# A graph kernel's first SAGE pass: two of eight blocks of adjacency rows multiplied by their mask on VectorE, and layer norm's scaling moved to ScalarE

## The chip, the cores and the metric

The kernel runs on 1 core of a Trainium2 chip. The time is that of one execution on the device, in microseconds (us). The engines are called as in the profile: PE is TensorE (matmuls; PEld its weight loads), DVE is VectorE, ACT is ScalarE, POOL is GpSimd, SP is SyncE, which here only issues transfers. Each engine works through its own instructions strictly in the order in which they are written; engines wait for each other through semaphores.

## The reference

Two graph layers are run on 16 graphs of 1024 nodes with 128 features. The first is a gated graph network of four steps. The second, cut to what matters:

```python
x = _layernorm(x + gated(x, adj, mask))       # end of the first layer
adj_d = adj * keep                            # keep: row by row, some neighbours are struck out, and their mirror images too
deg = clip(sum(adj_d, -1), 1)
out = (adj_d @ x / deg) @ Wr1 + x @ Wx1 + b1  # the first of three SAGE passes
h1  = batch_norm(relu(out / norm(out)))
# the sum adj_d @ h1 for the second pass is taken in the same sweep; two more passes and a head follow
```

adj holds zeros and ones. keep is stored as a matrix nr ("not removed") of zeros and ones, one for each graph, in which row i says what row i has struck out. Entry (i, j) of adj_d is 1 when adj, nr at (i, j) and nr at (j, i) are all 1.

## The kernel before

The program has four stages: the gated layer woven together with the search for removed neighbours (to about 1323 us), the first SAGE pass (Sage.first, about 1323 to 1893 us), the second pass, and the third pass with the head. The change is in the first pass alone.

The first pass walks over the graphs b in 16 slots each (method slot, t = 0 to 15), whose order is written out by hand; nothing is rescheduled. In one turn of 16 slots, graph n = b + 1 is prepared while graph b is multiplied. A batch here means one such turn. What a slot holds of the work that the prediction names:

- **unit(n, t)**, L1469, every slot. It makes a piece of 128 rows by 512 columns of the transposed adj_d. With f = t // 8 and j = t % 8, PE adds up in PSUM (p_u, two buffers) one 512-wide matmul of nr (L1477) and, for each of four row blocks k = 4f + i, a turned block of adj (L1483) and a turned block of nr (L1484), each a 128x128 bf16 matmul with the identity. ACT then writes relu(sum - 2) as p_at (L1485): 1 only where all three are 1. "Unit 8" is unit(n, 8), and "Relu 8" its L1485.
- **pack**, L1492: POOL casts each p_at to bytes (p_b).
- **agg**, L1556: eight 512-wide matmuls over p_at; for x in slots 0, 1, 3, 4, for the new features r in slots 9, 10, 12, 14.
- **evict**, L1562, ACT: in slots 2 and 5 the two sums over x leave PSUM (s_ag). "Evict 2" and "evict 5" below.
- **degrees**, slots 2 and 5: L1541 on DVE and L1542 on ACT read the degree row out of s_ag. **degree_columns**, slots 3 and 6: four tiny matmuls (L1549) turn it into PSUM tile s_tr, and DVE reads it there (L1551, L1552). s_tr has one buffer, so the next to write it waits for L1551.
- **out_first**, slots 5 and 7, PE; **scale_rows**, slots 6 and 8, DVE (L1376, L1377); **squares**, ACT (L1384, L1385); **rows**, slots 7 and 9, DVE (L1390 to L1395); **split**, ACT L1400 and POOL L1401; **turn_r**, slots 11 and 13, PE L1406, ACT L1592, DVE L1593.
- **norm_stats**, slots 0 and 1: DVE statistics of x of graph n (L1510, L1512), the root on ACT (L1515), the reciprocal on DVE (L1516). **norm**, slots 2 and 3: four DVE instructions each (L1522), x - mean times 1/deviation, in place. **turn_x**, slots 6 and 8: PE turns four blocks of x each into s_tr (L1406).
- **check(n, k)**, L1501: DVE tests that a block of adj holds only 0 and 1; each block is f32, 128x1024, and all of it is read. Blocks 4 to 7 in slots 4, 5, 10, 11, and blocks 0 to 3 of the graph after in slots 12 to 15.

Within a slot, what belongs to graph b is written ahead of what belongs to graph n, except unit. On DVE, slots 5 and 6 stand thus: L1541, the check of block 5, L1376, L1377, L1551, L1552. On PE, slot 6 is unit 6, L1549, turn_x, and the last waits for L1551.

Of the kernel before, what the change touches and what calls it, by code (L numbers as in the profile page):

```python
# [8 lines left out]
F32 = mybir.dt.float32  # L9
BF = mybir.dt.bfloat16  # L10
# [4 lines left out]
AF = mybir.ActivationFunctionType  # L15
ALU = mybir.AluOpType
# [5 lines left out]
P = 128  # L22
# [3 lines left out]
NB = N // P  # L26
# [357 lines left out]
def sage_layers(ctx, tc, cst, adj, mask, not_r, summed, x1, W, vec, Wl, bl, out):  # L384
# [106 lines left out]
    with ExitStack() as c1:  # L491
# [7 lines left out]
        for b in range(B):  # L499
# [3 lines left out]
            for f in range(2):  # L503
                t = nrp.tile([P, 4, N], BF, name="a_nr")
                nc.sync.dma_start(t, rows_of(not_r[b][f * HF:(f + 1) * HF, :]))
                nr.append(t)
            norm(s, s)
            nc.sync.dma_start(rows_of(x1[b]), s)
            ht = [transposed(lambda i: s[:, 4 * f + i, :], "s_t4",
# [70 lines left out]
    with ExitStack() as c3:  # L580
        ld = pool("c_ld", c3, bufs=2)
        psp = pool("c_psp", c3, bufs=2, space=PSUM)
        for b in range(B):
            s = ld.tile([P, NB, C], F32, name="c_x")
            nc.sync.dma_start(s, rows_of(x1[b]))
            ht = normed(b)
            project(2, b, ht, psp)
            for f in range(2):
                pt = ps2.tile([P, 4, P], F32, name="s_tr")
                for i in range(4):  # L590
                    nc.tensor.transpose(pt[:, i, :], acc[b][f][:, i * P:(i + 1) * P], ident)
                for i in range(4):
                    k = 4 * f + i
                    m = cst["mask"][:, k, b:b + 1]
                    y = wk.tile([P, C], F32, name="c_y")
                    nc.vector.scalar_tensor_tensor(y, pt[:, i, :], m, blb, op0=ALU.mult, op1=ALU.add)
                    nc.vector.scalar_tensor_tensor(s[:, k, :], y, m, s[:, k, :],
                                                   op0=ALU.mult, op1=ALU.add)
            norm(s, s)
            nc.sync.dma_start(rows_of(out[b]), s)  # L600
# [596 lines left out]
class Sage:  # L1197
# [14 lines left out]
    def __init__(self, ctx, tc, cst, adj, not_r, summed, nodemask, W, vec, Wl, bl, out, bad):  # L1212
# [27 lines left out]
        self.wxp = one.tile([C, 2, C], F32, name="s_wxp")  # L1240
        self.r6 = one.tile([6, 2 * C], BF, name="s_r6")

    def load_given(self):

        nc = self.nc
        nodemask, W, vec, Wl, bl = self.given
        for i in range(3):
            nc.sync.dma_start(self.wr[:, i, :], W[2 * i])
            nc.sync.dma_start(self.wx[:, i, :], W[2 * i + 1])
        nc.sync.dma_start(self.wl, Wl.rearrange("(k c) e -> c k e", c=C))  # L1250
        row = lambda v: v.rearrange("(o c) -> o c", o=1)
        for i, v in enumerate(vec):
            nc.sync.dma_start(self.vr[i:i + 1, :], row(v))
        nc.sync.dma_start(self.vr[9:, :], row(bl))
        self.m48 = self.wk.tile([P, NB, C], F32, name="p_rh", bufs=1).rearrange("p a b -> p (a b)")[:3 * B, :]
        for i in range(3):
            nc.sync.dma_start(self.m48[i * B:(i + 1) * B, :], nodemask)

    def constants(self):

        nc, ident, K = self.nc, self.cst["ident"], 3 * B
        const = self.const
        self.one16 = const([1, 1], 1.0, "s_one16", F16)

        self.sel01 = const([10, 3, 6], 0.0, "s_sel01")
        for i in range(3):
            nc.vector.tensor_copy(self.sel01[:, i, 3:], ident[:10, 3 * i:3 * i + 1].to_broadcast([10, 3]))
        self.ones = const([6, P], 1.0, "s_ones", BF)
        nc.vector.tensor_add(self.part6, ident[:6, 0:3], ident[:6, 3:6])
        self.part48 = const([K, 3], 1.0, "s_part48")  # L1270
        for base, m in ((0, 1), (B - 1, -1)):
            nc.gpsimd.affine_select(self.part48, self.part48, pattern=[[-m * B, 3]], compare_op=ALU.is_ge,
                                    fill=0.0, base=base, channel_multiplier=m)
        nc.vector.tensor_add(self.graph, ident[:K, :B], ident[:K, B:2 * B])
        nc.vector.tensor_add(self.graph, self.graph, ident[:K, 2 * B:K])
        nc.vector.memset(self.r6[:, C:], 0.0)

        mask, junk = self.cst["mask"], self.wxp[:, 0, :].rearrange("p (a b) -> p a b", a=NB)
        nc.vector.scalar_tensor_tensor(junk, mask, 0.0, mask, op0=ALU.is_gt, op1=ALU.not_equal,
                                       accum_out=self.bad[:, BAD - 1:BAD])  # L1280

        drop = self.wr2
        nc.vector.tensor_copy(drop, ident)
        nc.vector.memset(drop[:1, :], -1.0)
        nc.vector.memset(drop[:1, :1], 0.0)
        nc.vector.memset(self.mask48[:B, :], 1.0)
# [13 lines left out]
    def const(self, shape, v, name, dt=F32):  # L1300
        t = self.one.tile(shape, dt, name=name)
        self.nc.vector.memset(t.bitcast(F32) if dt is FR else t, v)
        return t
# [165 lines left out]
    def unit(self, b, t):  # L1469

        nc, g, f, j = self.nc, self.g[b], t // 8, t % 8
        if t == 0:
            g["at"] = self.atp[b % 2].tile([P, NB, N], FR, name="p_at")
        cols = slice(f * HF, (f + 1) * HF)
        ib, nr = self.cst["ident_b"], g["nr"]
        pu = self.ps2.tile([P, HF], F32, name="p_u")
        nc.tensor.matmul(pu, ib, nr[:, j, cols], start=True, stop=False)  # L1477
        for i in range(4):
            k = 4 * f + i

            a = g["a", k].bitcast(BF).rearrange("p (n h) -> p n h", h=2)
            blk = slice(j * P, (j + 1) * P)
            nc.tensor.matmul(pu[:, i * P:(i + 1) * P], a[:, blk, 1], ib, start=False, stop=False)  # L1483
            nc.tensor.matmul(pu[:, i * P:(i + 1) * P], nr[:, k, blk], ib, start=False, stop=(i == 3))  # L1484
        nc.scalar.activation(g["at"][:, j, cols], pu, AF.Relu, bias=self.less2)  # L1485
# [8 lines left out]
    def check(self, b, k):  # L1494

        if b >= B:
# [4 lines left out]
        self.nc.vector.scalar_tensor_tensor(low, a, 0.0, a, op0=ALU.is_gt, op1=ALU.not_equal,  # L1501
                                            accum_out=self.bad[:, c:c + 1])

    def norm_stats(self, b, f):
        nc, g = self.nc, self.g[b]
        if f == 0:
            g["mv"] = self.small.tile([P, NB, 2], F32, name="p_mv")
        st = self.small.tile([P, 4, 6], F32, name="p_st")
        for i in range(4):
            nc.vector.bn_stats(st[:, i, :], g["s"][:, 4 * f + i, :])  # L1510
        for i in range(4):
            nc.vector.bn_aggr(g["mv"][:, 4 * f + i, :], st[:, i, :])  # L1512
        if f == 1:
            g["rs"] = self.small.tile([P, NB], F32, name="p_rs")
            nc.scalar.activation(g["rs"], g["mv"][:, :, 1], AF.Sqrt, bias=self.eps)  # L1515
            nc.vector.reciprocal(g["rs"], g["rs"])  # L1516

    def norm(self, b, f):
        nc, g = self.nc, self.g[b]
        for i in range(4):  # L1520
            k = 4 * f + i
            nc.vector.tensor_scalar(g["s"][:, k, :], g["s"][:, k, :], g["mv"][:, k, 0:1], g["rs"][:, k:k + 1],  # L1522
                                    op0=ALU.subtract, op1=ALU.mult)

    def split_x(self, b, f):
        self.split(f, self.g[b]["s"][:, 4 * f:4 * f + 4, :], self.xh, self.xl, 1)
# [68 lines left out]
    def slot(self, b, t):  # L1595

        nc, g, n = self.nc, self.g.get(b), b + 1
# [23 lines left out]
        if now:  # L1621
# [3 lines left out]
            if t in (0, 1, 3, 4):  # L1625
                f, lo = t // 3, t in (1, 4)
# [5 lines left out]
            if t in (6, 8):  # L1632
                f = t // 8
# [3 lines left out]
            if t in (7, 9):  # L1637
                f = t // 9
# [15 lines left out]
        if nxt:  # L1654
            if t < 2:
                self.norm_stats(n, t)
            if t in (2, 3):
                self.norm(n, t - 2)
            if t in (6, 8):
                self.turn_x(n, t // 8)  # L1660
            if t in (7, 12):
                self.split_x(n, t // 12)
            if t < 4 and not now:
                self.check(n, t)
            if t in (4, 5, 10, 11):
                self.check(n, (4, 5, 10, 11).index(t) + 4)
            if t >= 12:
                self.check(n + 1, t - 12)

# [202 lines left out]
    def last(self, r48):  # L1872
        nc, tc, cst = self.nc, self.tc, self.cst
        with ExitStack() as c:
# [64 lines left out]
            for b in range(B + 1):  # L1939
                if b < B:  # L1940
                    head(b)
                if b:
                    norm(b - 1)
# [102 lines left out]
```

## Time and profile before

| | |
|---|---|
| median of 9 runs | 2365.28 us (2358.18 to 2365.91) |
| the profiled execution | 2363.19 us, of it the span from first to last instruction 2361.0 us |
| PE busy over the span | 96% |
| DVE, ACT, POOL busy over the span | 81%, 58%, 44% |
| the first SAGE pass | about 1323 to 1893 us |
| one steady batch of it (L1551 of slot 6 to the next) | 33.72 us |

All instruction times below are those of the one profiled execution; a line of the timeline gives start, duration, engine, source line, operation and tiles, and in brackets how long the engine had been idle and who released it. Durations on one engine overlap a little, so distances are taken from start to start.

### The profile page before, as it was taken

What the parts mean: (1) busy time and instruction counts of PE and PEld (TensorE: products, weight loads), DVE (VectorE), ACT (ScalarE), POOL (GpSimd) and SP (SyncE); (2) the same over time, 40 slices, a digit from 0 to 9 for tenths busy, and PEclk for the clock granted to TensorE, in tenths of its full rate; (3) what the DMA queues carried; (4) which work ended last, traced back from release to release, by engine and by line L of the source; (5) the groups of instructions that cost most, each with busy time, mean ns of one, the idle gap of its engine ahead of it and who ended that gap; (6) DMA issues with size and microseconds to landing.
All of it is one profiled execution on the core that took longest, in us unless ns stands there. A gap on an engine that the chain in (4) does not pass through costs nothing. (4 is left out here: it accounts for less than half of the span.)

```text
span 2361.0 us, 35730 instructions
## 1 busy us (share of the span) xinstructions
PE 2267.9 (96%) x11945; PEld 1563.4 (66%) x11945; DVE 1905.8 (81%) x4132; ACT 1371.7 (58%) x3206; POOL 1028.7 (44%) x964
## 2 busy tenths in 40 slices
PE   6999999999999999999999799999999999998987
PEld 4665655666656666656565577777777778886865
DVE  4998998998989989989899878777777566665777
ACT  3556565656465655555664565665666545555756
POOL 3235254263262452543532556666666435551002
PEclk9999999999999999999999899999999999998989
DMA  7327244363362362633640777778777277764414
GB/s 264 113 97 264 73 171 170 115 233 126 105 209 102 127 239 69 207 133 117 233 134 25 267 292 292 273 264 296 282 273 268 107 266 248 245 217 163 127 37 145
DMA packets 214406, 436.18 MB, mean 185 GB/s; under 512 B 59586, under 2 KB 80740, under 8 KB 214212
## 3 DMA queue, kind: packets, MB, share of 16 engines
q1 hardware_dynamic: 186244, 345.70, 42.0%
q0 software_dynamic: 23040, 83.90, 10.1%
q10 hardware_dynamic: 4928, 4.21, 0.6%
q8 instruction: 96, 1.57, 0.3%
q14 instruction: 98, 0.80, 0.1%
HBM read 324.49 MB, written 109.25 MB: 184 GB/s over the span
## 5 line engine op out<-in xcount | busy, mean ns | idle before, releaser
L1092 PE MATMUL h_g<-h_h,h_wh 128*128 128x512 f32 x768 | 397.8, 600 | 3.1 <-DVE h_r L1105 3.0
L1092 PE MATMUL h_g<-h_ms,h_wi 128*128 128x512 f32 x768 | 392.2, 592 | 0.0
L1492 POOL CAST p_b<-p_at 128x512 uint8<-128x512 f32 x256 | 258.0, 1028 | 121.8 <-ACT p_at L1485 121.8
L735 DVE TENSOR_TENSOR_SCAN f_rank<-f_a,f_first,f_pd 128x1024 f16<-128x1024 f32 x128 | 299.3, 2344 | 3.3
L1080 PE MATMUL h_g<-h_a,h_hi 128*128 128x512 f32 x1024 | 284.3, 418 | 5.9 <-DMA h_a<-in_adj_dram 5.7
L1092 PEld LDWEIGHTS h_g<-h_ms,h_wi 128*128 128x128 f32 x768 | 145.7, 190 | 183.8 <-issue 161.3
L1121 POOL TENSOR_TENSOR h_h<-h_zh,h_r 128x512 f32<-128x512 f32 x126 | 181.8, 1443 | 195.0 <-DVE h_r L1120 172.9
L1080 PE MATMUL h_g<-h_a,h_lo 128*128 128x512 f32 x1024 | 264.3, 395 | 0.0
L1485 ACT ACTIVATE p_at<-p_u,s_less 128x512 fp32r<-128x512 f32 x256 | 175.8, 688 | 145.9 <-PE p_u L1484 141.0
L1080 PEld LDWEIGHTS h_g<-h_a,h_hi 128*128 128x128 f32 x1024 | 188.5, 188 | 69.6 <-issue 20.1
L863 DVE SCALAR_TENSOR_TENSOR f_nr<-f_u,f_q,f_a 128x1024 bf16<-128x1024 f16 x128 | 183.8, 1453 | 57.1 <-ACT f_u L912 50.4
L1115 POOL TENSOR_TENSOR h_zh<-h_z,h_h 128x512 f32<-128x512 f32 x63 | 80.3, 1275 | 324.1 <-ACT h_z L1111 324.1
L1080 PEld LDWEIGHTS h_g<-h_a,h_lo 128*128 128x128 f32 x1024 | 190.1, 188 | 39.3
L1501 DVE SCALAR_TENSOR_TENSOR p_a<-p_a 128x1024 bf16<-128x1024 f32 x128 | 211.9, 1694 | 0.0
L1384 ACT ACTIVATE s_junk<-s_o 128x128 bf16<-128x128 f32 x384 | 113.8, 298 | 138.1 <-DVE s_o L1377 138.1
L1092 PEld LDWEIGHTS h_g<-h_h,h_wh 128*128 128x128 f32 x768 | 129.2, 191 | 86.2 <-issue 66.5
L1083 ACT COPY h_ms<-h_g 128x512 f32<-128x512 f32 x128 | 73.7, 576 | 174.8 <-PE h_g L1080 130.8
L1108 ACT ACTIVATE h_r<-h_r,h_bi 128x512 f32<-128x512 f32 x128 | 92.4, 722 | 138.8 <-DVE h_r L1107 138.8
L909 ACT ACTIVATE f_u<-f_rank,f_q 128x128 f16<-128x128 f16 (+7 forms) x128 | 110.5, 866 | 75.1 <-DVE f_rank L849 75.1
L1483 PE MATMUL p_u<-ident_b,p_a 128*128 128x128 bf16 x1024 | 144.6, 221 | 3.1 <-DMA p_a<-in_adj_dram 3.1
L1484 PE MATMUL p_u<-ident_b,p_nr 128*128 128x128 bf16 x1024 | 144.5, 221 | 0.0
L1763 PE MATMUL q_ob<-s_wxp,q_xt 128*128 128x256 f32 x512 | 133.0, 405 | 0.0
(258 smaller groups left out, 4944.0 us busy)
## 6 DMA issues: line engine op xcount, KB each, us to landing
h_a<-in_adj_dram POOLq DMA_DIRECT2D x128, 512.0 KB, 7.5
p_a<-in_adj_dram SPq DMA_DIRECT2D x128, 512.0 KB
f_a<-in_adj_dram SPq DMA_DIRECT2D x124, 512.0 KB
e_nr<-f_nr SPq DMA_DIRECT2D x128, 256.0 KB
p_nr<-e_nr SPq DMA_DIRECT2D x32, 1024.0 KB
s_at<-p_b SPq DMA_DIRECT2D x32, 512.0 KB
s_ag<-s_ag SPq DMA_DIRECT2D x64, 256.0 KB
q_agi<-s_ag SPq DMA_DIRECT2D x32, 512.0 KB
```

The lines of the kernel that those rows point to most:

```text
L735: nc.vector.tensor_tensor_scan(out, a, other[:, 0, 0:1].to_broadcast([P, N]), start, op0=ALU.add, op1=ALU.bypass)
L863: nc.vector.scalar_tensor_tensor(nr, self.us[g], self.q[:, 2, g:g + 1], self.a[g], op0=ALU.not_equal, op1=ALU.is_ge)
L1080: nc.tensor.matmul(pm[f], part[:, j, :], st.adj[j][:, half[f]], start=(j == 0 and n == 0), stop=(j == NB - 1 and n == 1))
L1092: nc.tensor.matmul(pg, lhs, rhs, start=(i == 0), stop=(i == len(mm) - 1))
L1121: aid.tensor_tensor(h, zh, r, ALU.subtract)
L1384: self.nc.scalar.activation(junk, o[:, i, :], AF.Square, accum_out=ss[:, i:i + 1])
L1483: nc.tensor.matmul(pu[:, i * P:(i + 1) * P], a[:, blk, 1], ib, start=False, stop=False)
L1484: nc.tensor.matmul(pu[:, i * P:(i + 1) * P], nr[:, k, blk], ib, start=False, stop=(i == 3))
L1485: nc.scalar.activation(g["at"][:, j, cols], pu, AF.Relu, bias=self.less2)
L1492: self.nc.gpsimd.tensor_copy(g["b", f][:, j, :], g["at"][:, j, f * HF:(f + 1) * HF].bitcast(F32))
L1501: self.nc.vector.scalar_tensor_tensor(low, a, 0.0, a, op0=ALU.is_gt, op1=ALU.not_equal, accum_out=self.bad[:, c:c + 1])
L1763: nc.tensor.matmul(pb[:, i], g["xt"][:, f, blk], self.wxp, start=False, stop=(i % 2 == 1))
```

## The change

For row blocks 4 and 5 of each graph (JOINED), DVE multiplies the block of adj by the same block of nr in place, in slots 5 and 6, behind that slot's check. Their units (slots 8 to 15) then need one turned matmul for such a block and not two: the product is turned with twice the identity, ident2, which is made once at the start of the pass. adj times nr counts double in the sum, which keeps relu(sum - 2) the same.

Layer norm's scaling goes from DVE to ACT: x times 1/deviation plus (-mean/deviation). norm_stats gets one more small DVE instruction for that offset, and norm is called in slots 2, 3, 4, 5 with two blocks each, where it was slots 2 and 3 with four each.

In the built program, PE has 256 matmuls and 256 weight loads fewer. On DVE, slots 5 and 6 now stand: L1541, the check of block 5, join of block 4, L1376, L1377, L1551, L1552, join of block 5. On ACT, a pair of scalings stands behind L1542 in slots 2 and 5, and behind the Relu in slots 3 and 4, the latter ahead of evict 5.

```diff
+    JOINED = 4, 5
...
+        self.ident2 = self.wxp[:, 1, :P // 2].bitcast(BF)
+        nc.vector.tensor_scalar(self.ident2, ident, 2.0, None, op0=ALU.mult)
...
             blk = slice(j * P, (j + 1) * P)
+            if k in self.JOINED:
+
+                nc.tensor.matmul(pu[:, i * P:(i + 1) * P], a[:, blk, 1], self.ident2, start=False, stop=False)
+                continue
             nc.tensor.matmul(pu[:, i * P:(i + 1) * P], a[:, blk, 1], ib, start=False, stop=False)
             nc.tensor.matmul(pu[:, i * P:(i + 1) * P], nr[:, k, blk], ib, start=False, stop=(i == 3))
...
+    def join(self, b, k):
+
+        a = self.g[b]["a", k]
+        self.nc.vector.tensor_mul(a, a, self.g[b]["nr"][:, k, :])
...
-            g["rs"] = self.small.tile([P, NB], F32, name="p_rs")
-            nc.scalar.activation(g["rs"], g["mv"][:, :, 1], AF.Sqrt, bias=self.eps)
-            nc.vector.reciprocal(g["rs"], g["rs"])
-
-    def norm(self, b, f):
-        nc, g = self.nc, self.g[b]
-        for i in range(4):
-            k = 4 * f + i
-            nc.vector.tensor_scalar(g["s"][:, k, :], g["s"][:, k, :], g["mv"][:, k, 0:1], g["rs"][:, k:k + 1],
-                                    op0=ALU.subtract, op1=ALU.mult)
+            rs = g["rs"] = self.small.tile([P, 2, NB], F32, name="p_rs")
+            nc.scalar.activation(rs[:, 0, :], g["mv"][:, :, 1], AF.Sqrt, bias=self.eps)
+            nc.vector.reciprocal(rs[:, 0, :], rs[:, 0, :])
+            nc.vector.scalar_tensor_tensor(rs[:, 1, :], g["mv"][:, :, 0], -1.0, rs[:, 0, :],
+                                           op0=ALU.mult, op1=ALU.mult)
+
+    def norm(self, b, m):
+
+        g = self.g[b]
+        for k in (2 * m, 2 * m + 1):
+            x = g["s"][:, k, :]
+            self.nc.scalar.activation(x, x, AF.Identity, bias=g["rs"][:, 1, k:k + 1],
+                                      scale=g["rs"][:, 0, k:k + 1])
...
-            if t in (2, 3):
+            if 2 <= t < 6:
                 self.norm(n, t - 2)
...
             if t in (4, 5, 10, 11):
                 self.check(n, (4, 5, 10, 11).index(t) + 4)
+            if t in (5, 6):
+                self.join(n, t - 1)
```

## Prediction

> **What bounds the kernel now.** The page first, for the engines' shares:
>
> ```profile
> PE 2267.9 (96%) x11945; PEld 1563.4 (66%) x11945; DVE 1905.8 (81%) x4132; ACT 1371.7 (58%) x3206; POOL 1028.7 (44%) x964
> ```
>
> PE is the busiest engine, but a share over the span says nothing of one stage. So next the busy times over two batches of the first pass, cut at L1551 of slot 6:
>
> ```profile
> core 0: us, PE busy (x) PEld busy (x) DVE busy (x) ACT busy (x) POOL busy (x), PEclk, DMA share, GB/s
> 1470.88:1504.61 33.73, 33.29 (x272) 26.22 (x272) 25.75 (x62) 20.81 (x50) 22.45 (x20) 1.00 0.77 279
> 1504.61:1538.33 33.72, 33.30 (x272) 26.23 (x272) 25.71 (x61) 20.80 (x50) 22.52 (x20) 1.00 0.77 283
> ```
>
> PE is busy 33.3 of 33.72 us at full granted clock; DVE has 8 us to spare, ACT 13. By sums, work taken from PE is time won. But the engines run in order and wait for each other several times a batch, so the timeline decides: first DVE, then PE, around slots 5 and 6.
>
> ```profile
> 1501.34 0.41 DVE L1541 TENSOR_SCALAR p_rho<-s_ag 1x512 bf16<-1x512 f32 x1 [0.44 <-ACT s_ag L1562]
> 1501.68 1.37 DVE L1501 SCALAR_TENSOR_TENSOR p_a<-p_a 128x1024 bf16<-128x1024 f32 x1
> 1502.96 0.09 DVE L1501 DVE_READ_ACCUMULATOR p_a<-p_a 128x1 f32 x1
> 1502.96 0.67 DVE L1376 TENSOR_TENSOR s_o<-p_oa,s_rdeg 128x512 f32<-128x512 f32 x1
> 1503.76 0.69 DVE L1377 TENSOR_TENSOR s_o<-p_ob,s_o 128x512 f32<-128x512 f32 x1
> 1504.61 0.16 DVE L1551 TENSOR_SCALAR s_rdeg<-s_tr 128x4 f32<-128x4 f32 x1
> ```
>
> ```profile
> 1504.82 0.66 PE L1406 MATMUL s_tr<-ident,p_s 128*128 128x128 f32 x4 [0.26 <-DVE s_rdeg L1551]
> ```
>
> DVE waits for evict 5 (0.44 us), then runs to L1551 with little air, and PE's turn_x already waits 0.26 us for L1551. This is where the join of block 4 goes in. Last ACT, slots 1 to 5 of the next batch:
>
> ```profile
> 1529.07 0.30 ACT L1515 ACTIVATE p_rs<-p_mv,s_eps 128x8 f32<-128x8 f32 x1 [1.91 <-DVE p_mv L1512]
> 1529.68 0.59 ACT L1562 COPY s_ag<-p_ag 128x512 f32<-128x512 f32 x1 [0.31 <-PE p_u L1484]
> 1530.17 0.70 ACT L1485 ACTIVATE p_at<-p_u,s_less 128x512 fp32r<-128x512 f32 x1
> 1530.75 0.60 ACT L1542 CAST p_rl<-s_ag 1x512 f16<-1x512 f32 x1
> 1531.26 0.67 ACT L1485 ACTIVATE p_at<-p_u,s_less 128x512 fp32r<-128x512 f32 x1
> 1532.56 0.69 ACT L1485 ACTIVATE p_at<-p_u,s_less 128x512 fp32r<-128x512 f32 x1 [0.62 <-PE p_u L1484]
> 1534.45 0.58 ACT L1562 COPY s_ag<-p_ag 128x512 f32<-128x512 f32 x1 [1.21 <-PE p_ag L1556]
> ```
>
> ACT is late here not by its own work: L1515 waits 1.91 us for DVE, which runs without a pause from L1593 of slot 11 (1517.05) through checks and statistics. From evict 2 to evict 5 ACT has 0.62 + 1.21 = 1.83 us of air, and six of the eight scalings go there.
>
> **What is removed from PE.** Two 128x128 bf16 matmuls in each of units 8 to 15. Such matmuls start 0.055 us apart (1362.39, 1362.45, 1362.50), so a unit loses 0.11 us: 256 x 0.055 = 14.2 us in the pass, 0.89 a batch. Unit 9's share is lost anyway: the agg behind it waits for the cast of p_rh on ACT (0.18 us now). Seven units count, 0.78 us a batch.
>
> **What is added: the join.** No row has it: f32 times bf16, 128x1024, both in SBUF. From below:
>
> ```profile
> L727 DVE TENSOR_TENSOR f_a<-f_a,f_tr 128x896 f32<-128x896 f32 x16 | 17.1, 1071 | 0.0
> L727 DVE TENSOR_TENSOR f_a<-f_a,f_tr 128x768 f32<-128x768 f32 x16 | 15.0, 938 | 0.0
> ```
>
> 128 more columns cost 133 ns, so 1024 take 1.20 us, less 0.08 of overlap with the next: 1.12. No row of two full tensors is faster, so nothing less is to be had. From above: a check alone starts the next instruction 1.28 us later; where POOL casts beside it, 1.69 (1523.50 to 1525.19), 0.41 more. POOL does cast here: p_b at 1502.15 takes 1.34 us, against 0.61 alone, and ends 0.53 us after the check. So 1.53 us is the other end. I take 1.53: checks beside casts are the nearest row, since the join too reads two SBUF tensors with a cast left waiting. The Trainium skill, "GPSIMD Engine Reference", section 1 (Specifications), says that POOL shares its SBUF interfaces with DVE, contended when a DVE instruction has two SBUF inputs; by it the join would pay (+11.1 us in the sum below), by the lone rows it would not (+5.4).
>
> The join of block 5 stands behind L1552 of slot 6, where DVE idles 1.56 us until ACT's L1385; cost nothing, and if that cover went, at most its surplus over 1.56, with unit 8 still 3 us away. Making ident2 falls into DVE's 2.71 us wait for p_s at the start. The one more 128x8 instruction behind L1516 costs about 0.2 us, in DVE's 0.4 to 0.7 us wait for evict 2.
>
> **What is moved: the scalings.** DVE loses eight (0.33 to 0.38 us), all ahead of its wait for evict 5, so that wait only grows: no gain. On ACT the head's own scaling is the same instruction:
>
> ```profile
> 2298.44 1.27 ACT L1930 ACTIVATE u_y<-u_y,u_rs 128x128 f32<-128x128 f32 x3
> 2299.62 1.47 ACT L1930 ACTIVATE u_y<-u_p,u_rs 128x128 f32<-128x128 f32 x4
> ```
>
> Three take 1.18 us start to start, 0.39 each, 0.79 a pair. Queued behind them: Relu 3, Relu 4, evict 5; for evict 5 waits DVE's L1541. The Trainium skill, "ScalarE: Activation LUTs", section "Rules for kernel authors", puts plain adds and multiplies on VectorE; it speaks against this move, and by it the scalings would stay where they were and the time would be that of the second case below.
>
> **The sum.** Follow one loop, start to start, from L1551 of slot 6 to the next:
> 1. L1551 to turn_x 0.21, unit 8 3.52, Relu 8 0.86, cast of p_rh 0.59, agg 0.65, unit 10 1.98, agg 0.65, unit 11 1.91, Relu 11 0.88, L1592 0.58, L1593 0.61: 12.44 us (1504.61 to 1517.05). Units 8, 10, 11 shorter by 0.11: 12.11.
> 2. L1593 to L1515: 12.02 (12.00 to 12.02 in three batches), DVE's checks and statistics, unchanged.
> 3. L1515 to evict 2: 0.34 (1461.62 to 1461.96).
> 4. Evict 2 to evict 5 on ACT: 0.49 to Relu 2, 0.58 to L1542, 0.51, pair 0.79, Relu 3 0.58, pair 0.79, Relu 4 0.58, pair 0.79: 5.11. Without the pairs 2.74, which is why PE set evict 5 before.
> 5. Evict 5 to L1541 0.62, check 0.34, join 1.28, then the join's own 1.53, L1376 0.61, L1377 0.61: 4.99. The small gaps before L1377 and L1551 (0.20 + 0.23) are used up.
>
> Together 12.11 + 12.02 + 0.34 + 5.11 + 4.99 = 34.57 us, against 33.72: **+0.85 us** a batch. With a join of 1.12, 34.16: +0.44. The loop before was some 31 us and hidden by PE; now it is longer than PE's work. From slot 6 of b = 0 to that of b = 14 are 14 loops: +11.9 (+6.2). Behind the last, seven units are still shorter: -0.8. At the start DVE loses norms from its full stretch and gains two joins; first_weights comes about 1.5 us earlier in b = 0, and its join takes that back: 0. Sum **+11.1 us** (+5.4). The four batches with a longer transfer wait (34.15 to 34.76 us) I leave as they are. The profiled execution took 2363.19 us: 2374.3. It lies 2.1 us under the median of the runs, and either may be met.
>
> **The rivals.**
> - **DVE's leg alone.** ACT has more air than I count, and only the join is in PE's way: it costs 1.12 - 0.43 = 0.69 to 1.10 us of PE wait against 0.78 won, so -0.09 to +0.32 a batch, -2 to +4 us: 2361 to 2367. For it: evict 5 would be late by only about 0.4 us. Against: PE's own lead over DVE's chain of step 2 shrinks with shorter units, so ACT starts later still.
> - **The join is hidden: faster.** If DVE reached L1551 in time, PE would keep nearly all: 2363.2 - 14.2 = 2349. It decides where the join fits into DVE's air between evict 5 and L1551, which is 0.43 us; a 1.1 us join doesn't. For it speaks only PE's 33.3 of 33.7.
> - **The join suffers more.** A check beside POOL's subtraction took 2.44 us. A join of 2.36 makes 35.40: +1.68 x 14 - 0.8 = +23, 2386. Against: in slot 5 POOL casts, it doesn't subtract.
> - That the change does less than it says is excluded on PE: the built program has the 256 matmuls fewer. A wait of 1 us does not cost PE its clock: after 0.96 us idle at 1566.25 the next unit ran as ever; waits of 3 to 5 us did (0.31 us matmuls for 0.22 at 1333).
>
> **How the numbers follow.** Forecast 0.64, DVE's leg alone 0.20, hidden 0.08, worse 0.08. The forecast's own range is 2368.6 to 2374.3, a little more with run-to-run spread. The range 2363 to 2380 takes in most of the second case, both ends of the join, and leaves out the third and fourth. 0.2% is 4.7 us, about what a measurement of this kernel can tell from no change: slower 0.72 (first and fourth case), same 0.20, faster 0.08.
>
> **What would show it.** In the profile after: a steady batch of 34.2 to 34.6 us from L1551 to L1551; PE's turn_x in slot 6 waiting 1 to 2 us for L1551; DVE's L1541 of slot 5 waiting longer for evict 5, and evict 5 no longer waiting for PE; a join of 1.2 to 1.6 us; scalings of 0.48 us on ACT. Wrong if the batch is under 33.5 us, if turn_x waits under 0.5 us, or if evict 5 still waits for PE.

## The result, and the profile after

The changed kernel takes **2373.93 us** (median of 9 runs, 2370.33 to 2375.82) against 2364.3 us for the kernel before (median of the 29 runs made with it): ratio **1.0041**, 95% interval [1.0030, 1.0052]. A second set of runs gave 2373.02 us against 2365.02, ratio 1.0033 [1.0020, 1.0046]. The forecast was 2374.3 us, slower.

Lines have moved: what was L1541, L1551, L1552 is now L1558, L1568, L1569; L1406 is L1411, L1485 is L1494, L1492 is L1501, the check L1501 is L1510, L1515 is L1529, L1562 is L1579. The join is L1516 and the scaling on ACT L1539.

First the engines' shares on the page, and the busy times in two clean batches (those in which evict 2 doesn't wait for a transfer), cut at L1568 of slot 6; both of the kernel after.

```profile
PE 2256.4 (95%) x11689; PEld 1551.2 (65%) x11689; DVE 1902.4 (80%) x4053; ACT 1415.8 (60%) x3334; POOL 1045.0 (44%) x964
```

```profile
1727.18:1761.21 34.03, 32.36 (x256) 25.32 (x256) 25.67 (x57) 23.46 (x57) 23.20 (x20) 1.00 0.75 277
1829.36:1863.39 34.03, 32.36 (x256) 25.31 (x256) 25.65 (x57) 23.46 (x57) 23.20 (x21) 1.00 0.56 203
```

PE has 0.94 us of work a batch less than before (33.30), and the batch is 0.31 us longer: PE now has 1.67 us of air in it, where it had 0.4. Where the air is, the timeline of PE and of DVE in slots 5 and 6 of the first of these batches says:

```profile
1761.42 0.66 PE L1411 MATMUL s_tr<-ident,p_s 128*128 128x128 f32 x4 [1.39 <-DVE s_rdeg L1568]
```

```profile
1757.11 0.41 DVE L1558 TENSOR_SCALAR p_rho<-s_ag 1x512 bf16<-1x512 f32 x1 [1.94 <-ACT s_ag L1579]
1757.45 1.33 DVE L1510 SCALAR_TENSOR_TENSOR p_a<-p_a 128x1024 bf16<-128x1024 f32 x1
1758.69 0.09 DVE L1510 DVE_READ_ACCUMULATOR p_a<-p_a 128x1 f32 x1
1758.69 1.21 DVE L1516 TENSOR_TENSOR p_a<-p_a,p_nr 128x1024 f32<-128x1024 f32 x1
1759.83 0.67 DVE L1381 TENSOR_TENSOR s_o<-p_oa,s_rdeg 128x512 f32<-128x512 f32 x1
1760.61 0.69 DVE L1382 TENSOR_TENSOR s_o<-p_ob,s_o 128x512 f32<-128x512 f32 x1
1761.21 0.15 DVE L1568 TENSOR_SCALAR s_rdeg<-s_tr 128x4 f32<-128x4 f32 x1
```

turn_x waits 1.39 us for DVE, where it waited 0.26. DVE waits 1.94 us for evict 5, where it waited 0.44, and then has the join between itself and L1568. ACT over the same slots:

```profile
1751.29 0.30 ACT L1529 ACTIVATE p_rs<-p_mv,s_eps 128x8 f32<-128x8 f32 x1 [2.39 <-DVE p_mv L1526]
1751.50 0.57 ACT L1579 COPY s_ag<-p_ag 128x512 f32<-128x512 f32 x1
1751.97 0.69 ACT L1494 ACTIVATE p_at<-p_u,s_less 128x512 fp32r<-128x512 f32 x1
1752.55 0.60 ACT L1559 CAST p_rl<-s_ag 1x512 f16<-1x512 f32 x1
1753.06 0.87 ACT L1539 ACTIVATE p_s<-p_s,p_rs 128x128 f32<-128x128 f32 x2
1753.84 0.66 ACT L1494 ACTIVATE p_at<-p_u,s_less 128x512 fp32r<-128x512 f32 x1
1754.41 0.86 ACT L1539 ACTIVATE p_s<-p_s,p_rs 128x128 f32<-128x128 f32 x2
1755.18 0.67 ACT L1494 ACTIVATE p_at<-p_u,s_less 128x512 fp32r<-128x512 f32 x1
1755.75 0.86 ACT L1539 ACTIVATE p_s<-p_s,p_rs 128x128 f32<-128x128 f32 x2
1756.52 0.56 ACT L1579 COPY s_ag<-p_ag 128x512 f32<-128x512 f32 x1
```

From evict 2 (1751.50) to evict 5 (1756.52) no line has a bracket: ACT works 5.02 us without a pause, and evict 5 no longer waits for PE. This is the loop that the prediction followed.

**Where the time went.** Four stretches add up to the span of an execution: to the start of the last constants built on POOL (a pair of affine selects); from there to the first L1568 of slot 6 ("the start"); 14 batches; the rest. The first profiled execution of the kernel after took 2380.19 us, 6 us over the median of its runs; a second one took 2372.11, and is the one to account with.

| us | to the last constants | start | 14 batches | rest | span |
|---|---|---|---|---|---|
| before | 1322.7 | 47.0 | 474.9 | 516.4 | 2361.0 |
| after, first profile | 1323.7 | 54.3 | 485.3 | 515.1 | 2378.5 |
| after, second profile | 1322.8 | 48.9 | 483.7 | 515.1 | 2370.4 |

In the second: 0.0 + 1.9 + 8.8 - 1.3 = +9.4 us; the medians differ by 9.6 us in the first set of runs and by 8.0 in the second. The 8.8 us of the batches are in two parts. Clean batches of 34.03 for 33.72 make 14 x 0.31 = 4.3 (the clean ones lie between 34.03 and 34.11). The other 4.5 are batches longer than a clean one: 7.2 us over the clean length in all (483.67 - 14 x 34.03), where before had 2.8. The waits name them. Of a window over 11 batches (1427 to 1793 us), before, after in the first profile and after in the second:

```profile
ACT s_ag L1562 <- DMA s_ag<-s_ag: 3.1, 5, 1.4
```

```profile
ACT s_ag L1579 <- DMA s_ag<-s_ag: 5.5, 9, 1.4
```

```profile
ACT s_ag L1579 <- DMA s_ag<-s_ag: 5.1, 8, 0.9
```

Columns are the sum, the number of waits and the longest. Evict 2 writes a buffer of s_ag that a store to DRAM must have left first. In the kernel before, such a wait cost less than it lasted: with one of 0.22 us the batch stayed at 33.73, with one of 1.44 it took 34.75. In the kernel after (second profile), one of 0.32 us made 34.49 and one of 0.90 made 35.09: each counts in full.

### The profile page after: what moved, and what is told of

It reads as the page before. It is cut to its first block, busy times and chain, and to the rows that moved or that the text cites. A ratio compares the mean times of both kernels' runs of the same rounds, so it can differ in the third digit from the quotient of the medians.

```text
span 2378.5 us, 35253 instructions
## 1 busy us (share of the span) xinstructions
PE 2256.4 (95%) x11689; PEld 1551.2 (65%) x11689; DVE 1902.4 (80%) x4053; ACT 1415.8 (60%) x3334; POOL 1045.0 (44%) x964
## 5 line engine op out<-in xcount | busy, mean ns | idle before, releaser
L1501 POOL CAST p_b<-p_at 128x512 uint8<-128x512 f32 x256 | 272.7, 1086 | 113.1 <-ACT p_at L1494 113.1
L1494 ACT ACTIVATE p_at<-p_u,s_less 128x512 fp32r<-128x512 f32 x256 | 175.6, 687 | 121.0 <-PE p_u L1493 118.8
L1510 DVE SCALAR_TENSOR_TENSOR p_a<-p_a 128x1024 bf16<-128x1024 f32 x128 | 210.8, 1686 | 6.3 <-DMA p_a<-in_adj_dram 6.3
L886 ACT ACTIVATE f_pd<-f_rank,f_q 128x128 f32<-128x128 f16 x128 | 59.1, 461 | 112.5 <-DVE f_q L697 109.2
L1492 PE MATMUL p_u<-ident_b,p_a 128*128 128x128 bf16 x768 | 116.3, 223 | 5.7 <-DMA p_a<-in_adj_dram 5.7
```

The source lines that it names most:

```text
L1501: self.nc.gpsimd.tensor_copy(g["b", f][:, j, :], g["at"][:, j, f * HF:(f + 1) * HF].bitcast(F32))
```

## The experiments

Each ran against the kernel before on the same chip (two chips in all), so runs are best compared by their ratios. The theory: the join and the scalings lie on one loop (ACT from evict 2 to evict 5, DVE from there to L1568, PE from there on), and this loop, not PE's work, is the batch. The rivals: one of the two edits alone is the cost; or the start is.

**Each edit alone.** Scalings on ACT, no joins:

```diff
-    JOINED = 4, 5
+    JOINED = ()
-            if t in (5, 6):
-                self.join(n, t - 1)
```

> Only the scalings move to ACT; no block is joined, all 2048 turned matmuls stay. Theory of the loop (DVE's stretch, ACT's pairs ahead of evict 5, the join, PE's turn_x, back to DVE): without the join the loop is 12.44 + 12.02 + 0.2 + 5.0 + 3.45 = 33.1 us, under PE's 33.72, so the steady batch stays 33.7 to 33.9 us and turn_x waits about 0.3 us for the degree columns: 2362 to 2367 us. Rival, ACT's pairs are the cost by themselves: evict 5 comes 0.3 to 0.4 us late and PE loses that in every batch, 34.1 us, 2369 to 2371 us. On the start of the pass the first theory says nothing beyond this: if POOL's casts starve there because DVE no longer has single-source scalings between its checks, the start is 5 us longer here too (2368 to 2371 us with a steady batch of 33.7); if it takes the joins of graph 0, it isn't.

Measured: 2363.9 us, ratio 0.9997 [0.9987, 1.0008]; clean batches 33.70. The start took 50.9 us in the profile (+3.9) and the time doesn't show it: the profile's batches took 472.5 us, 2.4 less than before.

Joins, with the scalings on DVE in slots 2 and 3 (norm and norm_stats as in the kernel before):

```diff
-            if 2 <= t < 6:
+            if t in (2, 3):
                 self.norm(n, t - 2)
```

> Blocks 4 and 5 joined as in the changed kernel; the scalings stay on DVE in slots 2 and 3. Theory of the loop: ACT's leg falls back to 2.74 us, so only DVE's leg is in PE's way: PE wins 0.78 us a batch and waits 1.13 - 0.43 = 0.70 us more for the degree columns, 33.6 to 33.7 us a batch, turn_x waiting about 1.0 us. Over 14 batches -1 us, and the start longer by the joins of graph 0 (units 8 to 15 wait for two joins behind four checks and eight scalings): 2363 to 2370 us. Rival, the join alone is the whole cost and ACT's pairs are hidden: a steady batch of 34.1 us or more, as in the changed kernel, 2370 to 2376 us.

Measured: 2372.5 us, ratio 1.0031 [1.0021, 1.0042]; a miss, some 2 us over the range. Clean batches were 33.75 to 33.79, so the loop did as expected, and the cost lies elsewhere: in the profile the start took 51.7 us (+4.7) and the 14 batches 478.5 (+3.6): the first of them was 2.1 us over a clean one, and most of the rest lies in batches with s_ag waits.

What follows: in a clean batch the scalings alone cost nothing (33.70 for 33.72) and the joins alone 0.05 us, but both together 0.31. The scalings alone stay under PE's work. The joins alone take 0.78 us from PE (the prediction's count) and make turn_x wait about 1.1 us (1.06 to 1.18), some 0.85 more than before. Together they lie end to end on one loop, and PE waits for the sum. And there is a second cost, of the start and of the s_ag buffers, that clean batches don't show. In time it is the larger one: the joins alone cost 7.6 us (2372.5 against 2364.94) with next to nothing lost in a clean batch.

**Graph 0 without joins.**

```diff
-            if k in self.JOINED:
+            if b and k in self.JOINED:
-            if t in (5, 6):
+            if n and t in (5, 6):
```

> The changed kernel, but graph 0, which is prepared alone at the start of the pass, is not joined: its units turn both blocks as before. If the 7 us that the profiled start lost come from unit 8 waiting for graph 0's joins, and from what queues behind them, the start is that of the kernel before and the time falls by 4 to 7 us, to 2367 to 2370 us; the steady batches stay at 34.1 us with longer ones among them. Rival, POOL's casts starve because DVE's checks follow one another without the scalings: the first byte store is still issued some 9 us late and the time stays at 2372 to 2376 us.

Measured: 2369.77 us, ratio 1.0019 [1.0007, 1.0032]. The start stays late, 51.0 us. After a first batch of 35.66 all batches are 34.05 to 34.10, with no wait for s_ag in the window. So the joins of graph 0 aren't all of the start's cost. The time is in the range of the theory, but for another reason: not the start became short, the s_ag waits are gone.

**The join in slot 4,** where DVE waits for evict 5:

```diff
-            if t in (5, 6):
-                self.join(n, t - 1)
+            if t in (4, 6):
+                self.join(n, 4 + t // 6)
```

> The changed kernel, with the join of block 4 one slot earlier, behind the check of block 4, where DVE waits about 2 us for evict 5; nothing else moves. Theory of the loop: the join leaves the way from evict 5 to the degree columns, the loop falls from 34.06 to 32.9 us and PE's own work (33.72 - 0.78 = 32.9 us) bounds again, so the steady batch is 32.9 to 33.3 us (the s_ag transfer, which ACT waits for at evict 2, may hold some batches up), turn_x waits 0.3 to 0.5 us: 14 batches of about -1.3 us against the changed kernel, 2356 to 2361 us. Rival, what costs is DVE's added work or its contention with POOL wherever the join stands: 2370 to 2376 us, as the changed kernel.

Measured: **2354.28 us, ratio 0.9958 [0.9943, 0.9974]**, faster than both kernels, and some 2 us under the range. Clean batches are 32.92 to 32.95: the 0.78 us that the prediction counted as saved on PE now come through. DVE's and PE's timeline show it, here from the run with a third buffer below (with two buffers, turn_x waits 0.26 to 0.29 us in the clean batches):

```profile
1537.30 1.47 DVE L1516 TENSOR_TENSOR p_a<-p_a,p_nr 128x1024 f32<-128x1024 f32 x1
1539.17 0.42 DVE L1558 TENSOR_SCALAR p_rho<-s_ag 1x512 bf16<-1x512 f32 x1 [0.40 <-ACT s_ag L1579]
1539.51 1.33 DVE L1510 SCALAR_TENSOR_TENSOR p_a<-p_a 128x1024 bf16<-128x1024 f32 x1
1540.76 0.09 DVE L1510 DVE_READ_ACCUMULATOR p_a<-p_a 128x1 f32 x1
1540.76 0.67 DVE L1381 TENSOR_TENSOR s_o<-p_oa,s_rdeg 128x512 f32<-128x512 f32 x1
```

```profile
1542.37 0.66 PE L1411 MATMUL s_tr<-ident,p_s 128*128 128x128 f32 x4 [0.26 <-DVE s_rdeg L1568]
```

The wait of 1.94 us for evict 5 has become a join of 1.47 and a wait of 0.40, and turn_x waits 0.26 us, as in the kernel before.

**A third buffer for s_ag,** in three kernels: the one after, the one before as control, and the one with the join in slot 4.

```diff
-        t = self.one.tile([C, HF], F32, name=f"s_ag{f}") if b == B - 1 else self.wk.tile([C, HF], F32, name="s_ag")
+        t = self.one.tile([C, HF], F32, name=f"s_ag{f}") if b == B - 1 else self.wk.tile([C, HF], F32, name="s_ag", bufs=3)
```

> The changed kernel with a third buffer for s_ag (bufs=3), so that evict 2 need not wait for the store of the aggregate two evictions earlier. Theory (the batches above the floor of 34.03 to 34.09 us are late transfers of s_ag, 5.5 us in 9 waits of 11 batches): the line of these waits is gone, the batches after the first stand at 34.0 to 34.1, their mean falls from 34.67 to about 34.2 (the first batch, 36.26, stays long), and the run comes out 14 x 0.47 = 6.5 us, at least 4 us, under the changed kernel: 2366 to 2370. Rival (the long batches come from the start, which leaves the units behind in phase, and the wait for the transfer only shows where the slack lies): the wait is gone by name, but another takes its place at evict 2, the batches keep 34.3 to 35.0 and the time stays at 2371 to 2376.

Measured: 2368.2 us, ratio 1.0019 [1.0007, 1.0030], so 0.0014 to 0.0022 less than without it (the intervals overlap). No wait for s_ag's transfer is left in the window; the batches are 35.54 and then 34.01 to 34.08.

> The kernel before with the same third buffer for s_ag, the control. Its batches above the floor of 33.72 sum to 34.76+34.35+34.37+34.15 minus 4 x 33.72 = 2.75 us. Theory: they fall to the floor, 2361 to 2363, ratio about 0.999; the gain is less than half of that of the changed kernel, since only 5 waits (3.1 us) were there. Rival (a third buffer only moves the transfers): no change within 0.05 per cent.

Measured: 2363.3 us, ratio 0.9993 [0.9982, 1.0005]; all batches 33.72 or 33.73. The batches did as the theory said, and the time can't be told from no change.

> The kernel with the first join moved from slot 5 to slot 4, with three s_ag buffers. Without the third buffer its floor was 32.92 to 32.95 us and its mean batch 33.47; waits for the transfer took 4.3 us in 8 batches of 11. Theory: the mean falls to 32.95 to 33.15 (the first batch stays long), 14 x 0.35 to 0.5 = 5 to 7 us less than 2354.3: 2347 to 2350. Rival (the long batches are a phase left by the start): 2352 to 2356.

Measured: 2353.79 us, ratio 0.9956 [0.9944, 0.9969]. The batches are 32.90 to 32.95 after a first of 35.78, 463.7 in all, against 468.6 with two buffers; but the time is the rival's, 0.5 us less. The profiled run with two buffers had been 10 us over its median; its start took 55.5 us, and its batches, too, may have been worse than the usual.

What follows: the waits of the long batches are for this buffer, shown by all three profiles, but for the first batch, which stays long in two of them (of that below). Their price in the medians is 3 to 5 us for the kernel after, and not measurable for the other two. Two buffers alone don't make these waits: with graph 0 not joined there was none in the window either, above and in the next run. How the start of the pass decides whether the stores come late, no run shows.

**The start.** Graph 0 as before (no join, scalings on DVE), the rest as in the kernel after:

```diff
     def norm(self, b, m):
         g = self.g[b]
+        if b == 0:
+            for k in range(4 * m, 4 * m + 4) if m < 2 else ():
+                x = g["s"][:, k, :]
+                self.nc.vector.tensor_scalar(x, x, g["mv"][:, k, 0:1], g["rs"][:, 0, k:k + 1],
+                                             op0=ALU.subtract, op1=ALU.mult)
+            return
...
-            if k in self.JOINED:
+            if b and k in self.JOINED:
-            if t in (5, 6):
+            if n and t in (5, 6):
```

> The changed kernel, with graph 0 treated as in the kernel before: its blocks not joined, and its eight scalings on DVE in slots 2 and 3. Two buffers of s_ag as in the changed kernel. Theory (the late start comes from DVE: with the scalings gone from it and joins added, it runs instructions with two operands in SBUF back to back and POOL's casts, the byte store behind them and the loads behind the store come late): POOL's first seven casts take 5 to 6.5 us instead of 16.1, the store waits about 4 us instead of 12.5, and the first division of batch 0 in slot 6 ends 46.3 us after the last constant is built as before, not 53.6; the time is about 7 us under the changed kernel: 2365 to 2368. With one part of it left out the start had been late by 4.6 us (scalings on ACT, no joins) and 5 us (joins, scalings on DVE). Rival (the start is late because of the loads' own transfers, or of the order on ACT): slot 6 stays at 51 to 54 us, time 2371 to 2375.

Measured: 2367.52 us, ratio 1.0018 [1.0009, 1.0027]. The start is 47.4 us, as before (47.0), and the casts are short again, as the theory said. Over all profiles the start stands for the four cases of graph 0: neither edit 47.0 to 48.6 (five profiles), scalings on ACT alone 50.9 and 51.0, joins alone 51.7, both 48.9 to 49.3 in four profiles and 54.3 and 55.5 in two (the first of the kernel after, and the join in slot 4 with two buffers). Two mechanisms are seen. POOL's first seven casts, of the kernel before, after in the second profile, scalings alone, and graph 0 as before:

```profile
1333.39 5.28 POOL L1492 CAST p_b<-p_at 128x512 uint8<-128x512 f32 x7 [8.42 <-ACT p_at L1485]
```

```profile
1332.94 11.35 POOL L1501 CAST p_b<-p_at 128x512 uint8<-128x512 f32 x7 [7.92 <-ACT p_rs L1529]
```

```profile
1333.98 11.30 POOL L1501 CAST p_b<-p_at 128x512 uint8<-128x512 f32 x7 [7.95 <-ACT p_at L1494]
```

```profile
1334.55 6.02 POOL L1501 CAST p_b<-p_at 128x512 uint8<-128x512 f32 x7 [7.82 <-ACT p_at L1494]
```

With the scalings on ACT, DVE runs check behind check here with nothing between them, and the casts take twice as long; with joins but DVE scalings they take 6.10 us. That the place of the scalings decides it is shown by one pair: graph 0 without joins has casts of 11.40 us and a start of 51.0, and with its scalings back on DVE, nothing else changed, 6.02 and 47.4. Behind the long casts SP's byte store waits 8 to 12 us (3.8 before), and the load of graph 1's fourth block behind the store is issued at about 1350 instead of 1344. Without joins PE then waits 6.6 us for that load. With joins, PE waits 4.0 to 8.2 us for L1516, and in most profiles about 1 us or less for the load: DVE at the start has no air for a join. In the two profiles with the long start PE waits for both, 4.0 and 4.6 us for L1516 and 5.7 and 4.6 for the load. Is the place of the store the harm? It was issued two slots later, in the kernel with the join in slot 4 and three buffers:

```diff
-            if t == 10:
+            if t == (10 if now else 12):
                 nc.sync.dma_start(self.at8[n, 0], self.g[n]["b", 0])
```

> First join in slot 4, three s_ag buffers, graph 0 changed like the others; only the first store of graph 0's bytes is issued two slots later (slot 12 instead of 10, for graph 0 alone), so that it stands behind the load of graph 1's fourth block and the first-stage weights in SP's queue instead of ahead of them. Theory (what makes the start late is this store, which waits 8 to 12 us for POOL's starved casts with that load behind it): the load is issued at about 1342 to 1345 instead of 1351, DVE's wait for it (3.6 us where only the scalings were moved) goes, and the start is 2 to 4 us shorter, 2350 to 2352.5, although the seven casts stay at 10 to 16 us. Rival (the casts themselves, or DVE's own order, set the start): no change, 2353 to 2355.

Measured: 2353.83 us, ratio 0.9952 [0.9940, 0.9964]: the rival's. The load came at 1340 and no engine waited for it, but the start took 48.9 us, since PE waited 4.8 us for the joins as before.

Then the same kernel with graph 0 as before, without and with the late store:

> First join in slot 4, three s_ag buffers, and graph 0 as in the kernel before (not joined, its scalings on DVE in slots 2 and 3). With graph 0 changed this kernel took 2353.8 us, batches of 32.90 to 32.95 after a first of 35.78, and 49.3 us from the last constant to the first division of slot 6; where graph 0 was left as before that stretch took 47.4 us, and 47.0 in the kernel before. Theory (DVE's two-operand instructions starve POOL at the start): POOL's first seven casts take 5 to 6.5 us instead of 11.3, the stretch about 47.4, so about 2 us less: 2351 to 2352.5; the batches stay as they are. Rival (the stretch is set elsewhere): 2353.5 to 2355.

Measured: **2348.75 us, ratio 0.9931 [0.9916, 0.9945]**, lower than either side had expected and the best of the study with the next.

> Both at once: graph 0 as in the kernel before and its first store issued two slots later. If the store ahead of the load is the whole harm of the late casts, little is left for either beside the other: the casts take 5 to 6.5 us, the store would have waited 4 us only, and the time is within 1.5 us of the better of the two, 2349.5 to 2352. If it is lower than both by over 2 us, the two act apart.

Measured: 2348.42 us, ratio 0.9930 [0.9915, 0.9945]: the place of the store is worth nothing beside it. Leaving graph 0 alone is worth 5 to 6 us (0.9931 against 0.9956), more than the start's 0.7 in the profiles (48.6 against 49.3). Most of the rest is in the first batch: 32.91 us for 35.78. From 1365 and from 1372 us on, with graph 0 joined and then without; the three last columns are the granted clock, the DMA share and GB/s:

```profile
1365.00:1372.00 7.00, 6.74 (x58) 5.24 (x58) 6.18 (x14) 4.01 (x8) 1.51 (x2) 1.00 0.95 337
1372.00:1380.00 8.00, 5.38 (x33) 4.53 (x32) 5.90 (x13) 3.84 (x13) 2.38 (x3) 0.64 1.04 398
```

```profile
1365.00:1372.00 7.00, 5.05 (x48) 3.98 (x46) 6.79 (x12) 4.00 (x8) 2.48 (x3) 1.00 1.05 396
1372.00:1380.00 8.00, 6.96 (x58) 5.86 (x59) 4.83 (x11) 6.05 (x25) 3.59 (x4) 1.00 0.70 258
```

The granted clock was 0.64 there in the one and 1.00 in the other. Over the whole first batch this holds in all fourteen profiles: in seven the clock was 0.91 or 0.95 and the first batch 1.5 to 2.9 us over the shortest one; in the other seven it was 1.00 and the first batch at most 0.6 us over, which an s_ag wait of 0.47 us goes with. Graph 0 doesn't decide it alone. The first batch of the kernel after with graph 0 as before, and of the one with the late store and graph 0 joined:

```profile
1371.83:1407.48 35.65, 33.95 (x256) 26.58 (x256) 25.73 (x57) 23.55 (x57) 22.98 (x20) 0.95 0.77 280
```

```profile
1373.62:1406.54 32.92, 32.31 (x255) 25.31 (x256) 25.95 (x58) 22.98 (x57) 21.82 (x19) 1.00 0.78 284
```

The second of these took 2347.92 us, the shortest of its six executions by 4 us, and its mean granted clock over the whole execution was 0.988, where the other five had 0.984 or 0.985. With graph 0 as before, six of the twelve executions of the last two kernels had 0.987 or more (2344.09 to 2347.80 us) and six 0.985 or 0.986 (2349.04 to 2353.11). So at a like clock leaving graph 0 alone is worth some 2 us, and the rest of the 5 to 6 comes with the clock. Whether it makes a low clock rarer, twelve and six executions don't show.

**The kernel after once more.**

> The changed kernel once more, as it is, for a second profile. Its first profiled run took 2380.2 us, 6 us above its median, and has 54.3 us from the last constant to the first division of slot 6, with POOL's first seven casts at 16.1 us; two kernels that differ from it only in a third s_ag buffer or the place of a join had 49.0 to 55.5 us and 11.0 us. If that length belongs to the kernel, it comes again, 53 to 55 us and 16 us; if it is an accident of one run, the stretch takes 49 to 51 us, the casts about 11 us, and the profiled time is nearer to the median of 2374. The batches above 34.1 us (s_ag transfers) should come again, not at the same places.

Measured: 2373.02 us; start 48.9, casts 11.35, mean batch 34.55, profiled time 2372.11. So 1.9 us of the start are the usual, and the other 5.4 of the first profile don't come in every execution: there the seven casts took 16.13 us, the load was issued at 1353.3, 29.6 us after the last constants (26.0 here), and PE waited 5.7 us for it. But it isn't a single accident either: the kernel with the join in slot 4 and two buffers also had its load 29.6 us after the constants and a start of 55.5, with casts of 10.95 us. What makes the load late in these two is open.

## Why the prediction was right

The loop it followed is there, and the number is right; but that the number is so near was luck. The loop was forecast at 11.9 us over the 14 batches and costs 4.3, less than the low end of 6.2; two terms that the prediction set at nothing, the s_ag waits and the start, make up for what the loop doesn't cost. Of its signs, turn_x, evict 5, the join and the scalings came as said; the clean batch, 34.03 us, lies under the 34.2 to 34.6.

- **The loop** (steps 1 to 5). Shown: the chain without a pause is in the trace, moving the join out of it takes 1.1 us off the batch, and moving the scalings out takes it to 33.77. The clean batch by steps, forecast and measured (1727.18 to 1761.21): steps 1 and 2 together 24.13 and 24.11; step 3 0.34 and 0.21; step 4 5.11 and 5.02; step 5 4.99 and 4.69. Sum 34.57 and 34.03.
- **The join, the term that was mis-sized.** "I take 1.53": it took 1.14 us start to start (1.21 long), the low end. That is 0.39 x 14 = 5.5 us too much. DVE didn't pay for POOL's company; POOL did. Its cast beside the check and the join, in the same batch:

```profile
1757.72 2.66 POOL L1501 CAST p_b<-p_at 128x512 uint8<-128x512 f32 x1 [1.20 <-ACT p_at L1494]
```

  2.66 us, where in the kernel before it took 1.34 beside the check alone:

```profile
1502.15 1.34 POOL L1492 CAST p_b<-p_at 128x512 uint8<-128x512 f32 x1 [0.82 <-ACT p_at L1485]
```

  In both the cast ends about 0.5 us after the start of the DVE instruction behind the check or the join (1760.38 and 1759.83; 1503.49 and 1502.96), near the 0.61 us that it takes alone: it looks as if it had waited for the two, which both read two SBUF tensors. What the Trainium skill says ("GPSIMD Engine Reference", section 1, Specifications), that the two engines contend for the SBUF interfaces when a DVE instruction has two SBUF inputs, agrees with that; this section doesn't say which of them is held up, and the prediction laid it on the wrong one. Against the step's other parts: the gap ahead of L1382, which the prediction counted as used up, stayed (L1381 to L1382 0.78 us, not 0.61).
- **"The four batches with a longer transfer wait I leave as they are."** Wrong by 4.5 us. Evict 2 heads the loop now, so a late transfer of s_ag lengthens the batch by all of its wait, and there were more of them (8 for 5 in the window). That they are what lengthens the batches is shown by the third buffer; why there were more is not shown.
- **The start, "0".** +1.9 us in the second profile, and more in some executions. The removal of work from DVE was counted as a gain of air; in fact the scalings had been the stretches in which POOL got on (casts of 5.28 us with them on DVE, 11.35 without), and PE waited 4.8 us for joins that nothing at the start hides.
- **The end,** -0.8: measured -1.3.
- Together: 14 x 0.31 + 4.5 + 1.9 - 1.3 = 9.4 us, forecast 11.1.
- **ACT for the scalings.** A pair takes 0.78 us (forecast 0.79). The rule that speaks against the move (the Trainium skill, "ScalarE: Activation LUTs", section "Rules for kernel authors") isn't borne out here by the move alone, at 0.9997 [0.9987, 1.0008]; beside the joins the clean batch with it is 0.26 to 0.29 us longer than without.
- **The rivals.** "DVE's leg alone" is the run with joins only: its clean batch, +0.05 us, fell into the forecast of -0.09 to +0.32, but its time of 2372.5 didn't fall into 2361 to 2367, for the start and s_ag again. "Hidden" came true as soon as the join stood where DVE waits. "The join suffers more" was nowhere seen in slot 5.

Open: what decides whether the first batch meets a lower granted clock, why the start is 5 us longer in some executions, and why the s_ag waits were absent where graph 0 wasn't joined.

## What to carry to other kernels

Two edits that each leave a steady batch as it was can lengthen it together when both lie on one chain between engines: add up the chain, not the engines' sums, and put added work into the wait that the other edit opens (here the join, one slot earlier: from 1.004 to 0.996). When a chain becomes the bound, look what else it waits for, buffers with stores in flight above all, since those waits now count in full. A steady batch isn't the whole time either: the joins alone left it as it was and still cost 7.6 us. Cost the first turn of a loop by itself: here DVE had no air in it yet, and the best kernel (0.993) leaves it as it was.

## What was not expected of the hardware

- DVE and POOL side by side on SBUF: the join (1.21 us) and the check ahead of it (1.33) went at nearly their own speed while a cast of 0.61 us alone took 2.66. Where DVE ran checks one behind another, seven casts took 11.3 us, and each check 1.75 instead of 1.26. So both can lose; which one does varied with what they met.
- The same code gave starts of 48.9 and 54.3 us in two executions, with casts of 11.4 and 16.1 us: one profile isn't enough to price a stretch in which DMA, POOL and DVE are all at work.
- The granted clock fell in some executions just behind the start, for 3 to 7 us, and the first batch was 1.5 to 2.9 us longer in each of these profiles and in no other.
